# Two-layer graph transformer on one Trainium2 core: two TensorE drains a round as the signal for its products, a new order of the round, gathers that wait only for buffers, and raw rows in layer 2

## The chip, the core and the metric

The kernel runs on one core of one Trainium2 chip. The metric is the device time of one launch in microseconds (us). Engines are named as in the profile: PE is TensorE's matmul, PEld its weight load, DVE is VectorE, ACT is ScalarE, POOL is GpSimd, SP is SyncE. A wait on "PE" below is a wait for a semaphore that a matmul counts up when it ends; a wait on "PE_sequencer" is a wait for one that a drain counts up. A drain is an instruction of TensorE's queue that ends when everything queued before it has ended.

## What is computed

A graph of 6250 nodes with 106250 edges, sorted by target. Two transformer convolutions with two heads of 64 columns, a batch norm with ReLU between them, then residual and layer norm. One convolution, cut to what matters:

```python
q, k, v = h @ Wq + bq, h @ Wk + bk, h @ Wv + bv          # (n, 2, 64)
e = edge_attr @ We                                        # edge_attr: cos(time) 32 | msg 64
alpha = (q[dst] * (k[src] + e)).sum(-1) / 8
a = segment_softmax(alpha, dst)
out = segment_sum((v[src] + e) * a, dst) + h @ Ws + bs
...
h = conv1(x); h = relu((h - mu) / sqrt(var + 1e-5) * bn_g + bn_b)
return layernorm(x + conv2(h))
```

All arithmetic is float32.

## The kernel before

The edges are cut into 105 chunks (NC) of 1024 edges (CE), each holding all edges of at most 64 nodes, so the softmax of a chunk needs nobody else. A chunk is one round of the loop in `conv(c, ...)`; `conv` runs twice, c = 0 for layer 1 and c = 1 for layer 2. `general` is a second program for other graphs, which does not run here.

The order of instructions on every engine is the order in which the Python code issues them (manual schedule). For chunk k the steps are:

- `fetch(k)`: SP loads the edge messages, the chunk's table of products with the queries (`ftab`) and, in layer 2, what layer 1 stored; DVE writes eight code columns (layer 1) or a column of ones (layer 2) into the chunk's tile `ff`. There are six such tiles (AHEAD + 2).
- `gather`: eight indirect DMAs of 128 rows each, issued by POOL, bring the source nodes' rows into `ff`: from `xv_d` in layer 1, in layer 2 from `h_d` (raw output of layer 1) for the first six chunks (RAW) and from `hn_d` (normalised, after ReLU) for the rest.
- `encode`, `sine`, `place` (layer 1): DVE and ACT make the time features; DVE copies them into `ff`.
- `turn_in(k, u)`: TensorE transposes one half of the chunk's rows (`fpx`, and in layer 1 the edge features, `fpe`), ACT copies them to SBUF (`fft`, `fet`).
- `score(k, u)`: two products for each half give the negative logits `fps`. `lowest`: DVE takes the minimum of both halves (`flow`) and the bias `fm`. `weigh`: ACT takes the exponential (`fs`).
- `turn_weights`: TensorE transposes `fs` (`fppt`), ACT copies to `fpt`. `gather_sums`: eight products sum the weighted rows (`fpa`).
- `divide` (DVE: `finv`, `fa`), `finish_turn` (two transposes, `fpo`, and a copy to `fat`), `apply` (products with Wv and We into `fpo`), `finish` (DVE adds the residual; `fres`).

One round k works on four chunks at once: score of k, weights and sums of k-1, division and result of k-2, transposes of k+1. Between the steps the loop pulls from a generator `extra` the side work: in layer 1 the table columns of the remaining twelve blocks of 512 nodes (one product `fpg` and its copy on ACT or DVE), then the rows of h; in layer 2 the tables and residuals of layer 2.

Every consumer waits for the count of the matmul that it needs, and some matmuls wait for PE's own count. Gathers are paced: `tick` is called behind chosen matmuls, and each call lets one gather of the queue go, which waits for that matmul; `allowed` bounds how far ahead. In layer 2 the code of `first_blocks` runs in rounds 0 to 2: it applies ReLU to twelve more blocks of h, transposes them and writes `hn_d`. From chunk 40 (SINGLE) on, layer 1 takes two chunks into one sine, so ACT loads its sine and exponential tables once for two rounds.

Of the kernel before, what the change touches and what calls it, by code (L numbers as in the profile page):

```python
# [1 line left out]

# [11 lines left out]
P = 128  # L14
# [484 lines left out]
class Plan:  # L499
    pass  # L500
# [63 lines left out]
def load_others(nc, pl, const, conv2, bn_g, bn_b):  # L564

    for i, (to, ap) in enumerate(pl.later):
        nc.sync.dma_start(to, ap)
        if i % 2:
            yield
    pl.bs2 = broadcast(nc, const, "fbs2", conv2["bs"], D)  # L570
    yield
    pl.bng = load_column(nc.sync, const, "fbng", bn_g)
    pl.bnb = load_column(nc.sync, const, "fbnb", bn_b)
    yield


def matrices(nc, pl, c, const, bank, brief=None):
# [3 lines left out]
    for i, w in enumerate((wq, wk, web)):  # L581
        pt = bank()
        nc.tensor.transpose(pt, w, pl.ident)
# [10 lines left out]
    for i, kt in enumerate((wkt, wett)):  # L594
        for h in range(H):
            r = slice(h * C, (h + 1) * C)
            pm = bank()
            nc.tensor.matmul(pm, wqt[r, :], kt[r, :], start=True, stop=True)
            a = const.tile([P, P], F32, name=f"fm{c}{h}{i}")
            nc.scalar.activation(a, pm, AF.Copy, scale=-1.0 / C ** 0.5)  # L600
            pb = bank()
            nc.tensor.matmul(pb[:, 0:1], kt[r, :], bq[r, :], start=True, stop=True)
# [22 lines left out]
def tables(nc, pl, c, fT, b0, work, bank):  # L625

    o = work.tile([P, GE, H, 3 - c], F32, name="fo", tag="fo", bufs=1)
    for i, (a, b) in enumerate(pl.mats[c]):
        pg = bank()
        nc.tensor.matmul(pg, a, fT, start=True, stop=True)  # L630
# [33 lines left out]
def ordered(ctx: ExitStack, tc: tile.TileContext, pl, x, dst, edge_attr_64, conv2, bn_g, bn_b, out):  # L664
# [12 lines left out]
    hn_d = dram.tile([N, D], F32, name="hn_d")  # L677
# [20 lines left out]
    SINGLE = 40  # L698

    RAW = 6  # L700

    WIDEN = range(SINGLE - 4, SINGLE)

    def conv(c, extra, first_blocks=None):
# [7 lines left out]
        p_tr = cs.enter_context(tc.tile_pool(name=f"fp_tr{c}", bufs=3, space=bass.MemoryType.PSUM))  # L712
        p_s = cs.enter_context(tc.tile_pool(name=f"fp_s{c}", bufs=3, space=bass.MemoryType.PSUM))
        p_a = cs.enter_context(tc.tile_pool(name=f"fp_a{c}", bufs=1, space=bass.MemoryType.PSUM))
        p_o = cs.enter_context(tc.tile_pool(name=f"fp_o{c}", bufs=1, space=bass.MemoryType.PSUM))
        pl.bank = lambda: p_tr.tile([P, GE], F32, name="fpg", tag="tr")
# [8 lines left out]
        def fetch(k):  # L725
# [16 lines left out]
            s.tab = load.tile([P, NN * H, 3 - c], F32, name="ftab")  # L742
            nc.sync.dma_start(s.tab, pl.tab_d[c][:, bass.ds(s.nb, NN)].rearrange("p n h w -> p (n h) w"))
            if c:
# [4 lines left out]
                s.r = load.tile([NN, D], F32, name="fr", bufs=AHEAD + 3)  # L749
                nc.sync.dma_start(s.r, res_d[bass.ds(s.nb, NN), :])  # L750

        queue = [(k, t) for k in range(NC) for t in range(T)]
        allowed = [-1, False]

        def gather(step):
            k, t = queue.pop(0)
            row = nc.gpsimd.indirect_dma_start(  # L757
                out=ch[k].f[:, t, (1 if c else 0):1 + D], out_offset=None,
                in_=(h_d if k < RAW else hn_d) if c else pl.xv_d,
                in_offset=bass.IndirectOffsetOnAxis(ap=pl.srcs[:, t, k:k + 1], axis=0))  # L760
            if step is not None:
                tc.add_manual_dep(row.ins, step.ins.name, together, reason="gathers keep to the pace of the chunks")
            ch[k].rows.append(row)

        def tick(step, extra=False):
            if queue and queue[0][0] <= allowed[0] and (allowed[1] or not extra):
                gather(step)

        shape = [P, T, TD]

        args, turned = [], []

        def encode(k):
# [3 lines left out]
            if not args:  # L777
                args.append(work.tile([P, 2, T, TD], F32, name="farg"))
            arg = args[0][:, len(args) - 1]
            args.append(k)  # L780
# [11 lines left out]

        def sine():
            arg, *of = args
            args.clear()
            z = work.tile([P, 2, T, TD], F32, name="fzs")
            nc.scalar.activation(z[:, :len(of)], arg[:, :len(of)], AF.Sin, bias=qpi)
            turned.extend((k, z[:, i]) for i, k in enumerate(of))
# [5 lines left out]
        def place():  # L804
            for k, z in turned:
                nc.vector.tensor_copy(ch[k].f[:, :, 1 + D:1 + D + TD], z)
                nc.sync.dma_start(enc_d[k].rearrange("p (t d) -> p t d", d=TD), z)
            turned.clear()

        def turn_in(k, u):  # L810
# [18 lines left out]
            if c:  # L829
                return  # L830
# [8 lines left out]
        def score(k, u):  # L839

            s = ch[k]
            if u == 0:
                s.ps = []
# [560 lines left out]
```

## Time and profile before

| | |
|---|---|
| Median of 3 runs | 2693.82 us (2690.7 to 2695.6) |
| The profiled execution: time, and span from first to last instruction | 2692.01 us, 2690.2 us |
| Mean granted TensorE clock | 0.953 |
| Busy share: PE, PEld, DVE, ACT, POOL | 87%, 64%, 50%, 47%, 60% |

A row of the timeline has the start from the span's beginning, the duration, the engine, the line, the operation, what it writes and reads, how many instructions were merged, and in brackets the engine's idle time ahead of it with what released it. "issue" there is time with no cause that the profile shows, "remote" a release whose sender it could not name. A row of a list of groups has line, engine, operation, tiles, count, then busy us and mean ns of one, then idle time before. A matmul's duration in a row includes the way through the array, so the step from one start to the next is the better measure of what it occupies.

### The profile page before, as it was taken

Reading aid. Unit: us, or ns where it says so; the run is one execution under the profiler, and the core shown is the slowest. Engines: PE = TensorE matmul, PEld = TensorE weight load, DVE = VectorE, ACT = ScalarE, POOL = GpSimd, SP = SyncE. Lnnn points to the kernel's source line nnn. Section 1 sums busy time; section 2 is a strip of 40 time slices with the busy share of each in tenths; the row PEclk is TensorE's granted clock in tenths of the full one; section 3 lists DMA queues with packets and bytes.
Section 4 is the critical chain, followed back from the end, with each engine's and each line's share of the span. In section 5 each row is a group of like instructions: output and inputs, shape, how many; then the busy total and the mean of one; then the engine's idle time right before and its main releaser. Section 6 shows DMA issues by size and latency. Waiting matters only on the chain. (4 is left out here: it accounts for less than half of the span.)

```text
span 2690.2 us, 40319 instructions
## 1 busy us (share of the span) xinstructions
PE 2330.4 (87%) x11482; PEld 1734.9 (64%) x11482; DVE 1331.9 (50%) x4153; ACT 1264.9 (47%) x2147; POOL 1618.3 (60%) x1701
## 2 busy tenths in 40 slices
PE   5898989899898999888957988888898889988887
PEld 3576767667676767767735666666666666666665
DVE  5566666566566666666535433333333333333233
ACT  3666666565555555545523343443334334333344
POOL 3666666666666666666245666666666666666661
PEclk8999999999999999999969999999999999999998
DMA  6455455545555455545365545555555555544451
GB/s 206 143 167 152 140 160 154 149 136 154 161 154 151 136 160 156 153 135 150 103 171 156 143 148 144 138 155 157 153 152 141 151 157 152 153 138 129 132 135 27
DMA packets 239234, 393.49 MB, mean 146 GB/s; under 512 B 62048, under 2 KB 156892, under 8 KB 235676
## 3 DMA queue, kind: packets, MB, share of 16 engines
q1 hardware_dynamic: 166302, 237.60, 29.7%
q0 software_dynamic: 54144, 112.01, 16.4%
q10 hardware_dynamic: 18558, 41.20, 4.3%
q8 instruction: 97, 1.59, 0.2%
q14 instruction: 133, 1.09, 0.1%
HBM read 274.66 MB, written 112.55 MB: 144 GB/s over the span
## 5 line engine op out<-in xcount | busy, mean ns | idle before, releaser
L757 POOL DMA_INDIRECT ff<-xv_d,fsrcs x840 | 808.3, 962 | 482.2 <-issue 172.9
L757 POOL DMA_INDIRECT ff<-hn_d,fsrcs x792 | 758.5, 958 | 434.2 <-issue 167.5
L880 PE MATMUL fpa<-ff,fpt 128*128 128x225 f32 x3360 | 743.0, 377 | 72.6 <-issue 36.9
L880 PEld LDWEIGHTS fpa<-ff,fpt 128*128 128x128 f32 x3360 | 667.7, 205 | 102.1 <-issue 45.4
L828 ACT COPY fft<-fpx 128x512 f32<-128x512 f32 x408 | 240.1, 589 | 627.6 <-PE fpx L820 144.3
L847 PE MATMUL fps<-fft,ftab 128*128 128x512 f32 x840 | 452.0, 620 | 3.1 <-issue 1.8
L854 DVE TENSOR_REDUCE flow<-fps 128x1 f32<-128x512 f32 x420 | 280.6, 685 | 282.4 <-PE fpa L880 99.0
L874 ACT COPY fpt<-fppt 128x512 f32<-128x512 f32 x420 | 228.5, 584 | 329.9 <-remote 71.6
L820 PE MATMUL fpx<-fident,ff 128*128 128x128 f32 x1680 | 263.5, 281 | 24.0 <-issue 15.8
L872 PEld LDWEIGHTS fppt<-fident,fs 128*128 128x128 f32 x1680 | 195.0, 141 | 134.2 <-issue 121.1
L862 ACT ACTIVATE fs<-fps,fm 128x512 f32<-128x512 f32 x420 | 267.4, 692 | 5.2 <-DVE fm L856 2.4
L820 PEld LDWEIGHTS fpx<-fident,ff 128*128 128x128 f32 x1680 | 202.5, 144 | 61.7 <-issue 43.9
L872 PE MATMUL fppt<-fident,fs 128*128 128x128 f32 x1680 | 224.5, 274 | 18.7 <-issue 15.2
L848 PE MATMUL fps<-fet,ftab 112*128 112x512 f32 x420 | 218.8, 602 | 0.0
L944 DVE SCALAR_TENSOR_TENSOR fres<-fpo,fr 64x128 f32<-64x128 f32 x105 | 29.4, 280 | 378.3 <-PE fps L847 107.0
L848 PE MATMUL fps<-fxT,ftab 112*128 112x512 f32 x420 | 216.0, 595 | 0.0
L847 PEld LDWEIGHTS fps<-fft,ftab 128*128 128x128 f32 x840 | 164.3, 227 | 56.6 <-issue 50.5
L903 PEld LDWEIGHTS fpo<-fident,fa 128*128 128x128 f32 x210 | 29.5, 141 | 254.9 <-issue 194.4
L903 PE MATMUL fpo<-fident,fa 128*128 128x128 f32 x210 | 61.9, 295 | 146.7 <-DVE fa L891 92.4
L848 PEld LDWEIGHTS fps<-fet,ftab 112*128 112x128 f32 x420 | 106.0, 253 | 78.3 <-issue 75.6
L835 ACT COPY fet<-fpe 112x512 f32<-112x512 f32 x210 | 124.3, 592 | 57.5 <-PE fpa L880 13.6
L833 PE MATMUL fpe<-fident,ff 128*112 128x128 f32 x840 | 130.4, 279 | 21.6 <-issue 12.9
(217 smaller groups left out, 2559.2 us busy)
## 6 DMA issues: line engine op xcount, KB each, us to landing
fmsg<-in_edge_attr SPq DMA_DIRECT2D x210, 256.0 KB
et_d<-fet SPq DMA_DIRECT2D x105, 448.0 KB
fxT<-et_d SPq DMA_DIRECT2D x105, 448.0 KB
ftab<-tab_d SPq DMA_DIRECT2D x105, 192.0 KB
tab_d<-fo ACTq DMA_DIRECT2D x13, 1536.0 KB
ff<-xv_d,fsrcs POOLq DMA_INDIRECT x840
enc_d<-fzs SPq DMA_DIRECT2D x105, 128.0 KB
ftab<-tab_d SPq DMA_DIRECT2D x105, 128.0 KB
```

The lines of the kernel that those rows point to most:

```text
L757: row = nc.gpsimd.indirect_dma_start(out=ch[k].f[:, t, (1 if c else 0):1 + D], out_offset=None, in_=(h_d if k < RAW else hn_d) if c else p ...
L820: turn = nc.tensor.transpose(px[:, t * P:(t + 1) * P], s.f[:, u * 4 + t, 1:1 + D], ident)
L828: nc.scalar.copy(s.ft[:, u * GE:(u + 1) * GE], px)
L833: turn = nc.tensor.transpose(pe[:EC, t * P:(t + 1) * P], s.f[:, u * 4 + t, 1 + D:], ident)
L835: nc.scalar.copy(s.et[:, u * GE:(u + 1) * GE], pe[:EC])
L847: tick(nc.tensor.matmul(ps, s.tab[:, :, 0], s.ft[:, w], start=True, stop=False))
L848: tick(nc.tensor.matmul(ps, s.tab[:EC, :, 1], s.et[:, w], start=False, stop=True), True)
L854: nc.vector.tensor_reduce(low[:, u:u + 1], s.ps[u], AX.X, OP.min)
L862: nc.scalar.activation(s.s[:, u * GE:(u + 1) * GE], s.ps[u], AF.Exp, bias=s.bias, scale=-1.0)
L872: turn = nc.tensor.transpose(pp[:, t * P:(t + 1) * P], s.s[:, at:at + P], ident)
L874: nc.scalar.copy(s.pt[:, u * GE:(u + 1) * GE], pp)
L880: add = nc.tensor.matmul(s.pa, s.pt[:, t * P:(t + 1) * P], s.f[:, t, 1:1 + D + EW], start=t == 0, stop=t == T - 1)
```

## The change

Four parts, all in `conv` and the generators that it pulls:

1. **Signals.** Each product of TensorE is put into a group (`put`). `drained()` issues a drain and declares it the fence of that group: whoever needs one of these products waits for the drain. There are two a round: one behind `turn_weights(k-1)` and `score(k)`, one behind `turn_in(k+1)` and `finish_turn(k-2)`. The PSUM tiles are fixed: four banks used in turn for transposes and side products, two for scores.
2. **Order of the round.** Both halves of each step stand together. Reading and writing of PSUM are split (`copy_weights`, `copy_in`, `keep_turned`), so copies stand behind the drain. `finish` moves to round k+3, `gather_sums` and `apply` to the round's end. Each side product has one more `yield` between the product and its copy, and the loop pulls twice where it pulled once.
3. **Gathers.** `gather(k + 4)` issues all eight at the top of round k; they wait for the tile `ff` alone. `tick`, `allowed`, SINGLE and WIDEN go. Each chunk has its own sine.
4. **Raw rows.** All chunks of layer 2 gather from `h_d`. ACT applies scale, shift and ReLU as it copies `fft`; DVE's `normalise` runs for all 105 chunks, as two operations (multiply by scale, maximum with -shift) where it was three for six chunks. The missing shift is put back once through the last row of the edge weights. `hn_d`, `relu` and `first_blocks` go; ReLU of a block stands in `block`.

```diff
+        def put(product):
+            group.append(product)
+            return product
+
+        def drained():
+            drain = nc.tensor.drain()
+            name = f"products{c}_{next(fences)}"
+            for product in group:
+                tc.add_to_no_dep_group(name, product.ins)
+            tc.declare_fence(drain.ins, group=name)
+            group.clear()
...
-        def gather(step):
-            k, t = queue.pop(0)
-            row = nc.gpsimd.indirect_dma_start(
-                out=ch[k].f[:, t, (1 if c else 0):1 + D], out_offset=None,
-                in_=(h_d if k < RAW else hn_d) if c else pl.xv_d,
-                in_offset=bass.IndirectOffsetOnAxis(ap=pl.srcs[:, t, k:k + 1], axis=0))
-            if step is not None:
-                tc.add_manual_dep(row.ins, step.ins.name, together, reason="gathers keep to the pace of the chunks")
-            ch[k].rows.append(row)
+        def gather(k):
+            for t in range(T):
+                ch[k].rows.append(nc.gpsimd.indirect_dma_start(
+                    out=ch[k].f[:, t, (1 if c else 0):1 + D], out_offset=None, in_=h_d if c else pl.xv_d,
+                    in_offset=bass.IndirectOffsetOnAxis(ap=pl.srcs[:, t, k:k + 1], axis=0)))
...
-            for i, op in enumerate((OP.mult, OP.add)):
+            for i, op in enumerate((OP.mult, OP.max)):
                 nc.vector.tensor_tensor(rows, rows, pl.spread[:, None, i].to_broadcast([P, T, D]), op)
-            nc.vector.tensor_scalar(rows, rows, 0.0, None, op0=OP.max)
...
                 if on(k + AHEAD):
                     fetch(k + AHEAD)
-                if k == -3:
-                    for _ in range(T + T // 2 if c else 2 * T):
-                        gather(None)
...
+                    gather(k + AHEAD)
...
+                pulls = 0 if k < 0 else 2 if k < 4 or k > 96 else 1
+                if c == 0 and on(k + 1):
+                    place(k + 1)
                 if on(k - 1):
                     turn_weights(k - 1)
...
+                if on(k):
+                    score(k)
+                if group:
+                    drained()
+                if c == 0 and k > 0:
+                    pull()
+                if on(k - 1):
+                    copy_weights(k - 1)
                 if on(k - 2):
                     divide(k - 2)
...
+                if on(k - 3):
+                    finish(k - 3)
                 if on(k):
                     lowest(k)
+                    weigh(k)
+                if on(k + 1):
+                    turn_in(k + 1, 0)
+                    turn_in(k + 1, 1)
+                if c and pulls:
+                    pull()
                 if on(k - 2):
                     finish_turn(k - 2)
+                if group:
+                    drained()
+                if on(k - 2):
+                    keep_turned(k - 2)
                 if on(k + 1):
...
+                    copy_in(k + 1, 0)
+                    copy_in(k + 1, 1)
+                if c and pulls:
+                    pull()
+                if on(k + 2):
+                    settle(k + 2)
+                if c and on(k):
+                    normalise(k)
+                    place(k)
+                if c == 0 and on(k + 2):
+                    encode(k + 2)
                 if on(k - 1):
                     gather_sums(k - 1)
...
                 if on(k - 2):
                     apply(k - 2)
...
+                if c == 0 and pulls:
+                    pull()
```

Three places of the new order. In the rows, a bracket names the semaphores that the instruction waits for (DMASW: gathers, DMAHW: other DMAs; drains have no row of their own).

**TensorE, a round of layer 2 without side work.** Before:

```order
L872 MATMUL fppt<-fident,fs 128x128 [waits PE_49,Activation_49]
L872 MATMUL fppt<-fident,fs 128x128 x3
L872 MATMUL fppt<-fident,fs 128x128 [waits PE_49,Activation_49]
L872 MATMUL fppt<-fident,fs 128x128 x3
L847 MATMUL fps<-fft,ftab 128x512 [waits Activation_49]
L848 MATMUL fps<-fxT,ftab 128x512
L903 MATMUL fpo<-fident,fa 128x128 [waits DVE_49,PE_49]
L904 MATMUL fpo<-fident,fa 128x128
L820 MATMUL fpx<-fident,ff 128x128 [waits DMASW4_49,DMASW5_49,DMASW3_49,DMASW6_49,DMASW2_49,DMASW7_49,DMASW1_49,DMASW0_49]
L820 MATMUL fpx<-fident,ff 128x128 x3
L880 MATMUL fpa<-ff,fpt 128x225 [waits Activation_49]
```

With the change (fpx and fppt are now the banks ftr; the first drain stands behind the second L864, the second behind L919 and its twin):

```order
L888 MATMUL ftr_13833<-fident,fs 128x128 [waits Activation_49]
L888 MATMUL ftr_13833<-fident,fs 128x128 x3
L888 MATMUL ftr_13830<-fident,fs 128x128 [waits Activation_49]
L888 MATMUL ftr_13830<-fident,fs 128x128 x3
L863 MATMUL fps_13834<-fft,ftab 128x512 [waits DMAHW5_49,Activation_49]
L864 MATMUL fps_13834<-fxT,ftab 128x512 [waits DMAHW7_49]
L863 MATMUL fps_13835<-fft,ftab 128x512 [waits Activation_49]
L864 MATMUL fps_13835<-fxT,ftab 128x512
L834 MATMUL ftr_13831<-fident,ff 128x128 [waits DMASW4_49,DMASW5_49,DMASW3_49,DMASW6_49,DMASW2_49,DMASW7_49,DMASW1_49,DMASW0_49]
L834 MATMUL ftr_13831<-fident,ff 128x128 x3
L834 MATMUL ftr_13832<-fident,ff 128x128 x4
L919 MATMUL fpo<-fident,fa 128x128 [waits DVE_49]
```

TensorE no longer waits for its own count, both halves of the scores follow each other, and the transposes of `fa` come behind all transposes of the next chunk.

**VectorE and ScalarE, a round of layer 1.** VectorE before, from the division to the copy of `fpo`:

```order
L888 TENSOR_SCALAR finv<-fpa 128x1
L889 RECIPROCAL finv<-finv 128x1 [waits DVE_49]
L891 TENSOR_SCALAR fa<-fpa,finv 128x225 [waits DVE_49]
L854 TENSOR_REDUCE flow<-fps 128x1 [waits PE_49] x2
L856 TENSOR_SCALAR fm<-flow 128x1 [waits DVE_49]
L906 COPY fat<-fpo 128x256 [waits PE_49]
```

With the change:

```order
L758 TENSOR_SCALAR ff<-fbits 128x8x8 [waits PE_sequencer_49,DVE_49]
L759 CAST ff<-fbits 128x8x8
L820 COPY ff<-fzs 128x8x32 [waits Activation_49]
L905 TENSOR_SCALAR finv<-fpa 128x1
L906 RECIPROCAL finv<-finv 128x1 [waits DVE_49]
L908 TENSOR_SCALAR fa<-fpa,finv 128x225 [waits DVE_49]
L949 TENSOR_TENSOR fres<-fpo,ftab 64x64 [waits DMAHW7_49]
L949 TENSOR_TENSOR fres<-fpo,ftab 64x64
L870 TENSOR_REDUCE flow<-fps_504 128x1
L870 TENSOR_REDUCE flow<-fps_505 128x1
L872 TENSOR_SCALAR fm<-flow 128x1 [waits DVE_49]
L925 COPY fat<-fpo 128x256 [waits PE_sequencer_49]
```

The first drain of the round is awaited by the code columns of `fetch` (their tile was read by the last `gather_sums`), and `fetch`, `place` and `finish` now stand ahead of the minimum. ScalarE before, in the later part of layer 1:

```order
L874 COPY fpt<-fppt 128x512 [waits PE_49,Activation_49]
L874 COPY fpt<-fppt 128x512 [waits PE_49]
L828 COPY fft<-fpx 128x512 [waits PE_49,Activation_49]
L835 COPY fet<-fpe 112x512 [waits DMAHW3_49,PE_49,Activation_49]
L862 ACT_TABLE_LOAD
L862 ACTIVATE fs<-fps,fm 128x512 [waits DVE_49]
L862 ACTIVATE fs<-fps,fm 128x512
```

With the change:

```order
L894 COPY fpt<-ftr_500 128x512 [waits PE_sequencer_49,Activation_49]
L894 COPY fpt<-ftr_501 128x512
L878 ACT_TABLE_LOAD [waits DVE_49]
L878 ACTIVATE fs<-fps_504,fm 128x512 [waits Activation_49]
L878 ACTIVATE fs<-fps_505,fm 128x512
L853 COPY fft<-ftr_502 128x512 [waits PE_sequencer_49,Activation_49]
L854 COPY fet<-ftr_503 112x512 [waits DMAHW4_49,Activation_49]
L853 COPY fft<-ftr_500 128x512
L854 COPY fet<-ftr_501 112x512
L812 ACT_TABLE_LOAD [waits DMAHW7_49,DVE_49]
L812 ACTIVATE fzs<-farg,qpi 128x256 [waits Activation_49]
```

The exponential's table load now carries the wait for VectorE's bias `fm`, so it starts after it; it stands in every round.

**POOL, gathers of layer 2.** Before, and with the change:

```order
L757 DMA ff<-hn_d,fsrcs 128x128 [waits DMASW2_49,PE_49]
L757 DMA ff<-hn_d,fsrcs 128x128 [waits DMASW3_49,DVE_49,PE_49]
L757 DMA ff<-hn_d,fsrcs 128x128 [waits DMASW4_49,PE_49]
L757 DMA ff<-hn_d,fsrcs 128x128 [waits DMASW5_49,PE_49]
L757 DMA ff<-hn_d,fsrcs 128x128 [waits DMASW6_49,PE_49]
```

```order
L772 DMA ff<-h_d,fsrcs 128x128 [waits DMASW2_49]
L772 DMA ff<-h_d,fsrcs 128x128 [waits DMASW3_49,PE_sequencer_49,DVE_49]
L772 DMA ff<-h_d,fsrcs 128x128 [waits DMASW4_49]
L772 DMA ff<-h_d,fsrcs 128x128 [waits DMASW5_49]
L772 DMA ff<-h_d,fsrcs 128x128 [waits DMASW6_49]
```

One gather of eight waits for a drain, the other seven only for the gather that used their semaphore last.

257 lines of the change are left out of this document (126 added, 131 removed).

## The prediction

> **What bounds the kernel now.** I read the timeline of TensorE first, for the length of a round, then the timeline of all engines around a stall, then the same in a stretch without gathers, then the groups by line for durations. `gather_sums` occurs once a round, so its first row of each layer and its last give the rounds:
>
> ```profile
> 85.85 3.21 PE L880 MATMUL fpa<-ff,fpt 128*128 128x225 f32 x16
> ...
> 1341.79 3.21 PE L880 MATMUL fpa<-ff,fpt 128*128 128x225 f32 x16
> ...
> 1408.02 4.29 PE L880 MATMUL fpa<-ff,fpt 128*128 128x225 f32 x11
> ...
> 2667.53 4.89 PE L880 MATMUL fpa<-ff,fpt 128*128 128x225 f32 x16
> ```
>
> 104 steps each: layer 1 takes (1341.79 - 85.85)/104 = 12.08 us a round, layer 2 (2667.53 - 1408.02)/104 = 12.11. What TensorE needs is less. Near the end of layer 1, where no side work is pulled, its starts are:
>
> ```profile
> 1317.38 3.21 PE L880 MATMUL fpa<-ff,fpt 128*128 128x225 f32 x16
> 1320.42 0.60 PE L820 MATMUL fpx<-fident,ff 128*128 128x128 f32 x4
> ...
> 1321.29 0.39 PE L913 MATMUL fpo<-fat,fwv 128*128 128x128 f32 x2
> ...
> 1321.74 1.08 PE L847 MATMUL fps<-fft,ftab 128*128 128x512 f32 x2
> 1322.66 1.02 PE L848 MATMUL fps<-fet,ftab 112*128 112x512 f32 x2
> 1323.52 1.04 PE L872 MATMUL fppt<-fident,fs 128*128 128x128 f32 x8
> 1324.40 1.08 PE L847 MATMUL fps<-fft,ftab 128*128 128x512 f32 x2
> ...
> 1327.27 3.21 PE L880 MATMUL fpa<-ff,fpt 128*128 128x225 f32 x16
> ```
>
> From start to start: sums 3.04, eight transposes 0.87, `apply` 0.45, a product with 512 columns 0.92 or 0.86, eight transposes of weights 0.88; the whole round 1327.27 - 1317.38 = 9.89. So some 2 us of each round are not work. The next stretch shows what they are:
>
> ```profile
> 1893.39 1.04 PE L872 MATMUL fppt<-fident,fs 128*128 128x128 f32 x8
> ...
> 1893.94 0.28 DVE L944 SCALAR_TENSOR_TENSOR fres<-fpo,fr 64x128 f32<-64x128 f32 x1 [5.24 <-PE fppt L872]
> ...
> 1896.29 0.63 PE L820 MATMUL fpx<-fident,ff 128*128 128x128 f32 x4
> ...
> 1899.75 1.07 ACT L874 COPY fpt<-fppt 128x512 f32<-128x512 f32 x2 [4.10 <-remote]
> 1899.84 0.69 DVE L854 TENSOR_REDUCE flow<-fps 128x1 f32<-128x512 f32 x1 [2.33 <-remote]
> 1899.93 0.95 POOL L757 DMA_INDIRECT ff<-hn_d,fsrcs  x1 [1.63 <-remote]
> 1900.39 1.87 PE L880 MATMUL fpa<-ff,fpt 128*128 128x225 f32 x4 [3.47 <-issue]
> ```
>
> The transposes of the weights ended at 1893.39 + 1.04 = 1894.43, and ACT, idle, copies them at 1899.75, 5.3 us later. ACT, DVE and POOL are released together within 0.2 us, while TensorE has stood since 1896.92 waiting for that copy. Nobody worked: the matmuls' counts came late and in one burst. Where no gathers run, they do not:
>
> ```profile
> 1304.75 1.07 ACT L874 COPY fpt<-fppt 128x512 f32<-128x512 f32 x2 [2.42 <-PE fps L847]
> 1304.79 0.94 POOL L757 DMA_INDIRECT ff<-xv_d,fsrcs  x1 [1.35 <-PE fps L847]
> ...
> 1305.11 0.16 DVE L888 TENSOR_SCALAR finv<-fpa 128x1 f32<-128x1 f32 x1
> ...
> 1305.50 0.45 DVE L891 TENSOR_SCALAR fa<-fpa,finv 128x225 f32<-128x225 f32 x1
> ...
> 1305.87 1.28 DVE L854 TENSOR_REDUCE flow<-fps 128x1 f32<-128x512 f32 x2
> ...
> 1307.18 0.21 DVE L856 TENSOR_SCALAR fm<-flow 128x1 f32<-128x1 f32 x1
> ...
> 1308.25 1.28 ACT L862 ACTIVATE fs<-fps,fm 128x512 f32<-128x512 f32 x2
> ...
> 1310.52 0.60 PE L820 MATMUL fpx<-fident,ff 128*128 128x128 f32 x4
> ...
> 1311.16 0.59 ACT L828 COPY fft<-fpx 128x512 f32<-128x512 f32 x1 [1.62 <-PE fpx L820]
> ```
>
> The gather at 1304.79 is the last of layer 1. After it the transposes end at 1311.12 and ACT copies at 1311.16, 0.04 us later, and the rounds run at 9.89. So the kernel is bound by TensorE's signals being held while POOL gathers; ACT's signal came at once even in the burst (the first copy ends near 1900.29, TensorE starts at 1900.39).
>
> **The change part by part.** *Signals.* A drain's signal is not in this trace. Its delay lies between 0.04 (no gathers) and 5.3 us (the stall). I take 0.05, because it is TensorE's queue and not the matmul that counts, and the other engines' counts, like ACT's above, are not held; both ends stay for the range. The drain itself costs TensorE the way through the array that otherwise overlaps (L848: 1.02 long, next start 0.86 later, so 0.16) and a restart (0.1, as at 1900.39): 0.26, with the signal about 0.3. Below zero it cannot be, since a drain does no work; above, I allow 0.65, one whole product of 512 columns (0.59) waited out. By the Trainium skill (PSUM — Partial Sum Buffer, Engine vs sequencer instructions) a drain is a true completion signal because it waits for the engine to go fully idle; no run here shows one yet, and by that rule the 0.16 is paid each time and nothing can hide it.
>
> *Order, layer 1.* The groups by line of layer 1 give the other durations:
>
> ```profile
> L862 ACT ACT_TABLE_LOAD x68 | 87.2, 1283 | 1.2
> L931 DVE TENSOR_TENSOR fres<-fpo,ftab 64x64 f32<-64x64 f32 x194 | 49.5, 255 | 105.6 <-PE fppt L872 35.5 <-PE fps L847 29.1 <-PE fpo L914 14.8
> L806 DVE COPY ff<-fzs 128x256 f32<-128x256 f32 x98 | 29.1, 323 | 59.6 <-ACT fzs L797 35.8 <-issue 23.5
> L634 ACT ACTIVATE fo<-fpg,fb 128x512 f32<-128x512 f32 x22 | 25.9, 1175 | 7.3 <-PE fppt L872 4.9 <-PE fpg L630 2.2 <-PE fps L847 0.2
> L740 DVE TENSOR_SCALAR ff<-fbits 128x64 f32<-128x64 int32 x97 | 25.7, 265 | 3.3
> L741 DVE CAST ff<-fbits 128x64 f32<-128x64 int32 x97 | 24.6, 254 | 0.0
> ```
>
> From the first drain's signal (0), for which the code columns now wait with all of DVE's round queued behind them: DVE does code columns 0.27 + 0.25, place 0.32 (0.9 with the latency), divide 0.84 (1305.11 to 1305.95; 1.75), finish 2 x 0.26 (2.3), minimum 1.28 and bias 0.21 (3.8). Only then ACT loads its table, 1.28 (5.15), and takes two exponentials, 1.28 (6.45). TensorE: four transposes, then twelve more once place is done at 0.9 (2.3); `finish_turn` writes the PSUM tile that `finish` reads, so it waits for 2.3 and ends at 2.6; second drain, 2.85; sums 3.04 (5.9), apply (6.35), weights 0.88 (7.2; the exponential allows 6.95), scores 2 x 1.78 (10.75), drain: 11.0. The second drain's consumers are late anyway (ACT is in the exponential until 6.45), so its signal costs nothing. A side product adds 0.92: 11.9. Its copy now stands ahead of the rest: on ACT 1.18 ahead of the weights' copies, whose two banks the last edge transposes need again (0.6 more, since TensorE reaches them 0.6 before), on DVE about the same length ahead of divide (1.1 more). A block of twelve takes seven rounds: 11.9, 12.5, 12.5, 13.0, 13.0, 12.1 and 11.0, mean 12.3; the other twenty rounds, with the rows of h, I put at 11.6 between 11.0 and 12.3. Layer 1: 12.15, which is 104 x 0.07 = 7 us more. The extra sine table load each round lies behind the copies on ACT, which has ended by then (6.45 + 4 x 0.59 = 8.8 of 11).
>
> *Order, layer 2.* No code columns, no table: divide is done at 0.95, fres (0.28) at 1.25, `finish_turn` ends near 1.6, drain 1.85, sums 4.9, apply 5.4, weights 6.3 (the exponential ends at 4.8), scores 9.8, drain 10.0. A side product adds 0.92 less the wait for fres that it fills: 10.5. Sixty of 105 rounds have one: 10.3. The copies for layer 2 lie behind ACT's and DVE's work of the round and have 3 us of room.
>
> *Gathers and raw rows.* POOL, when nothing holds it, and beside `normalise`:
>
> ```profile
> 1357.32 0.94 POOL L757 DMA_INDIRECT ff<-h_d,fsrcs  x1 [0.30 <-issue]
> 1358.57 0.95 POOL L757 DMA_INDIRECT ff<-h_d,fsrcs  x1 [0.30 <-issue]
> ...
> 1397.63 1.62 POOL L757 DMA_INDIRECT ff<-h_d,fsrcs  x1 [10.10 <-PE fps L847]
> ...
> 1422.54 2.49 DVE L896 TENSOR_TENSOR ff<-ff,fspread 128x1024 f32<-128x1024 f32 x2
> ...
> 1423.40 1.19 POOL L757 DMA_INDIRECT ff<-h_d,fsrcs  x1 [0.30 <-issue]
> ```
>
> One gather each 1.25 us makes 8 x 1.25 = 10.0 a round, now a floor close to TensorE's 10.3. What DVE does in layer 2 today, in a table of stretches (length; then busy us and count of PE, PEld, DVE, ACT, POOL; clock, DMA share, GB/s):
>
> ```profile
> 1660.00:1960.00 300.00, 264.72 (x1303) 190.41 (x1302) 108.75 (x371) 114.78 (x239) 189.61 (x199) 0.95 0.54 151
> ```
>
> DVE is busy 108.75 of 300, or 4.4 of 12.11 us a round. `normalise` adds 2.49, which leaves it at 6.9 of 10, and lengthens a gather beside it by 0.24 (1.19) to 0.67 (1.62): 10.2 to 10.7. I take 10.5 for layer 2, which is 104 x (12.11 - 10.5) = 167 us less. `first_blocks` goes with it; its rounds are in the 12.11. The spare work (a later `finish`, start, change of layers) I leave at nothing, with 10 us either way.
>
> Sum against the profiled span: 2690.2 + 7 - 167 = 2530; the profiled run's time was 1.8 above its span and the median of the runs 1.8 above that: 2534, said as **2530**.
>
> **The rivals.** *Slower: the drain's signal is held like the matmul's.* All DVE and ACT work and, through place or fres, TensorE hang on the first drain, so a mean delay h costs 208 x h. It decides from h = 160/208 = 0.8 us; at 1.5, 2845. For it: SP, DVE, ACT and POOL all saw TensorE late; against: only matmuls were seen to count late. *POOL is shut out during `normalise`*: 10.0 + 2.49 = 12.5 in layer 2, 104 x 0.4 = 41 us more, 2740; the rows above lengthen by a quarter of that. The Trainium skill (SBUF — State Buffer, SBUF: two separate sides) states that rule, an exclusive lock between GpSimd and two-input VectorE work; the trace agrees only in part, 0.24 and 0.67 of 2.49. *Drains cost 0.65*: 416 x 0.35 = 146 more, 2675. *Layer 1's copies are hidden after all*: 11.0 + 0.92 x 5/7 x 0.8 = 11.5, 70 us less, 2460. *The signals change nothing*, because gathers themselves slow the round: 2690.
>
> **How the numbers follow.** Forecast 45%, held signals 17%, hidden copies 15%, dear drains 12%, shut-out POOL 6%, nothing 5%. Runs of this kernel tell 0.2% from no change. Faster: 45 + 15 + 10 = 70%; within 0.2%: 3%; slower: 17 + 6 + 4 = 27%. The range 2410 to 2745 leaves out most of the held signals and the end of the hidden copies. The forecast's own range is 2480 to 2590.
>
> **What would show it.** Right: copies start within 0.2 us of a drain, no releases "remote" after TensorE has ended; rounds of 11 to 13 us in layer 1 and 10 to 10.7 in layer 2; POOL idle 0.30 between gathers. Wrong: idle ACT and DVE for over 0.8 us after a drain's last product, or gathers of over 1.2 us throughout layer 2.

## The result, and the profile after: slower by 9%

| | before | after |
|---|---|---|
| Median, us | 2692.26 (4 runs) | 2949.28 (4 runs, 2927.61 to 2958.13) |
| Ratio, 95% interval | | 1.0943 [1.0879, 1.1007] |
| Profiled execution: time, span, clock | 2692.01, 2690.2, 0.953 | 2954.61, 2952.6, 0.932 |

Forecast was 2530, between 2410 and 2745. The rounds first, from the timeline of TensorE of the kernel after: the first product of `gather_sums` (now L900) in the first and last round of each layer.

```profile
124.53 0.45 PE L900 MATMUL fpa<-ff,fpt 128*128 128x225 f32 x1
...
1456.10 0.46 PE L900 MATMUL fpa<-ff,fpt 128*128 128x225 f32 x1
...
1548.66 0.45 PE L900 MATMUL fpa<-ff,fpt 128*128 128x225 f32 x1
...
2931.19 0.45 PE L900 MATMUL fpa<-ff,fpt 128*128 128x225 f32 x1
```

The start takes 124.5 in place of 85.9 (+39), a round of layer 1 12.80 in place of 12.08 (+75 over 104), the change of layers 92.6 in place of 66.2 (+26), a round of layer 2 13.29 in place of 12.11 (+123), the end 1 less: +262, the whole difference of the spans. The lower mean clock is no cause of its own: the step from one score product to the next is 0.43 us in both traces. Every stage that was to stay got longer, and layer 2 with them.

The groups of the page after (line, engine, operation, count; busy and mean; then idle time ahead and what ended most of it; L782 is the drain):

```profile
PE 2390.7 (81%) x11435; PEld 1735.1 (59%) x11435; DVE 1506.5 (51%) x4336; ACT 1363.5 (46%) x2240; POOL 1637.3 (55%) x1701
...
L772 POOL DMA_INDIRECT ff<-h_d,fsrcs x840 | 825.9, 983 | 647.5 <-DVE finv L906 324.7
...
L894 ACT COPY fpt<-ftr 128x512 f32<-128x512 f32 x420 | 226.5, 591 | 845.9 <-PEq L782 779.2
...
L905 DVE TENSOR_SCALAR finv<-fpa 128x1 f32<-128x1 f32 x210 | 31.4, 150 | 544.6 <-issue 528.0
...
L758 DVE TENSOR_SCALAR ff<-fbits 128x64 f32<-128x64 int32 x105 | 21.4, 204 | 436.4 <-PEq L782 434.3
```

ACT and DVE wait for the drain, and POOL for DVE's first steps behind it. A wait for a drain is no fault by itself; what matters is when TensorE's last product had ended. A steady round of layer 2, from the timeline of all engines:

```profile
1897.14 0.94 POOL L772 DMA_INDIRECT ff<-h_d,fsrcs  x1 [2.27 <-DVE finv L906]
...
1906.10 0.94 POOL L772 DMA_INDIRECT ff<-h_d,fsrcs  x1 [0.30 <-issue]
...
1906.53 1.02 PE L864 MATMUL fps<-fxT,ftab 112*128 112x512 f32 x2
...
1908.73 0.15 DVE L905 TENSOR_SCALAR finv<-fpa 128x1 f32<-128x1 f32 x1 [4.99 <-issue]
...
1908.77 1.07 ACT L894 COPY fpt<-ftr 128x512 f32<-128x512 f32 x2 [6.31 <-PEq L782]
...
1909.21 1.06 PE L834 MATMUL ftr<-fident,ff 128*128 128x128 f32 x8 [1.66 <-DMA ff<-h_d,fsrcs]
1909.42 0.94 POOL L772 DMA_INDIRECT ff<-h_d,fsrcs  x1 [2.37 <-DVE finv L906]
...
1911.08 0.27 PE L920 MATMUL fpo<-fident,fa 128*128 128x128 f32 x1
...
1911.43 2.96 PEld L900 LDWEIGHTS fpa<-ff,fpt 128*128 128x128 f32 x16 [0.31 <-issue]
...
1911.69 0.41 DVE L925 COPY fat<-fpo 128x256 f32<-128x256 f32 x1
```

The first drain's last product ends at 1906.53 + 1.02 = 1907.55; DVE, ACT and TensorE itself go on at 1908.7 or later. (The row of TensorE names a DMA, but the rows of that chunk were gathered three rounds earlier.) The second drain, two gathers into the next train, lets TensorE go on 0.08 us after its product (1911.35). The eight gathers start from 1897.14 to 1906.10; the signal comes 2.6 us after the last start, the next train 0.7 after the signal: 8.96 + 2.6 + 0.7 = 12.3, and 1909.42 - 1897.14 = 12.28. The train holds the signal that lets the next train go. In layer 1 the same drain comes 2.84 us after the train's last start and is not late:

```profile
507.57 0.94 POOL L772 DMA_INDIRECT ff<-xv_d,fsrcs  x1 [0.30 <-issue]
...
509.39 1.02 PE L864 MATMUL fps<-fet,ftab 112*128 112x512 f32 x2
...
510.47 1.07 ACT L894 COPY fpt<-ftr 128x512 f32<-128x512 f32 x2 [2.96 <-PEq L782]
```

Where a train gets longer than eight, the hold can too. In six rounds of layer 2 the second drain falls into a train of eleven or twelve and is held 3.1 to 10.3 us. The longest of these holds (the last product ends at 2195.84 + 0.27 = 2196.11):

```profile
2195.84 0.27 PE L920 MATMUL fpo<-fident,fa 128*128 128x128 f32 x1
...
2202.97 0.94 POOL L772 DMA_INDIRECT ff<-h_d,fsrcs  x1 [0.30 <-issue]
...
2206.49 0.43 DVE L925 COPY fat<-fpo 128x256 f32<-128x256 f32 x1 [9.99 <-PEq L782]
...
2206.51 5.93 PE L900 MATMUL fpa<-ff,fpt 128*128 128x225 f32 x16 [10.40 <-issue]
```

And at the start of layer 1 the first 48 gathers, which wait for nothing, follow each other: ACT's first copy starts 37.8 us after its transposes ended at 67.79.

```profile
66.73 1.06 PE L842 MATMUL ftr<-fident,ff 128*112 128x128 f32 x4
...
105.58 0.58 ACT L853 COPY fft<-ftr 128x512 f32<-128x512 f32 x1 [40.98 <-PEq L782]
```

The trace records the end of every drain; the end of a product in a trace is modelled, but in runs where nothing is held (below) every drain ends 0.02 to 0.05 us behind it. From the end of the last product ahead of it, the 457 drains of this kernel took 293 us, 84 of them over 1 us; 302 took under 0.1. Count as one train the gathers that start within 2 us of each other: of 186 drains whose last product ended among the first five gathers of a train, none took over 0.25 us; of 61 that came later in one, 48 took over 0.3. Of all 113 that took over 0.3 us, 94 ended 2.25 to 3.0 us after a train's last start; eight ended before it, among them two of the longest, 11.7 and 14.1 us, in the 48 gathers at the change of layers.

### The profile page after: what moved, and what is told of

Read it like the earlier page. It is cut to its first block, busy times and chain, and to the rows that moved or that the text cites. A ratio compares the mean times of both kernels' runs of the same rounds, so it can differ in the third digit from the quotient of the medians.

```text
span 2952.6 us, 39328 instructions
## 1 busy us (share of the span) xinstructions
PE 2390.7 (81%) x11435; PEld 1735.1 (59%) x11435; DVE 1506.5 (51%) x4336; ACT 1363.5 (46%) x2240; POOL 1637.3 (55%) x1701
## 5 line engine op out<-in xcount | busy, mean ns | idle before, releaser
L772 POOL DMA_INDIRECT ff<-h_d,fsrcs x840 | 825.9, 983 | 647.5 <-DVE finv L906 324.7
L900 PE MATMUL fpa<-ff,fpt 128*128 128x225 f32 x3360 | 751.1, 380 | 96.9 <-issue 81.7
L900 PEld LDWEIGHTS fpa<-ff,fpt 128*128 128x128 f32 x3360 | 664.7, 203 | 163.1 <-issue 145.8
L894 ACT COPY fpt<-ftr 128x512 f32<-128x512 f32 x420 | 226.5, 591 | 845.9 <-PEq L782 779.2
L834 PE MATMUL ftr<-fident,ff 128*128 128x128 f32 x1680 | 254.8, 287 | 256.8 <-DMA ff<-h_d,fsrcs 128.5
L834 PEld LDWEIGHTS ftr<-fident,ff 128*128 128x128 f32 x1680 | 191.8, 146 | 420.3 <-issue 405.4
L913 DVE TENSOR_TENSOR ff<-ff,fspread 128x1024 f32<-128x1024 f32 x210 | 256.3, 1221 | 3.6
L888 PE MATMUL ftr<-fident,fs 128*128 128x128 f32 x1680 | 230.2, 280 | 13.5 <-issue 11.6
L888 PEld LDWEIGHTS ftr<-fident,fs 128*128 128x128 f32 x1680 | 188.0, 142 | 60.4 <-issue 41.9
L864 PE MATMUL fps<-fxT,ftab 112*128 112x512 f32 x420 | 217.2, 598 | 0.7 <-issue 0.7
L864 PE MATMUL fps<-fet,ftab 112*128 112x512 f32 x420 | 216.3, 596 | 0.0
L851 ACT ACTIVATE fft<-ftr,fshift,fscale 128x512 f32<-128x512 f32 x210 | 152.0, 781 | 101.0 <-PEq L782 99.2
L925 DVE COPY fat<-fpo 128x256 f32<-128x256 f32 x210 | 87.5, 417 | 140.5 <-PEq L782 134.3
L842 PE MATMUL ftr<-fident,ff 128*112 128x128 f32 x840 | 132.5, 281 | 23.8 <-DVE finv L905 11.6
```

What stands on the lines that cost most here:

```text
L772: ch[k].rows.append(nc.gpsimd.indirect_dma_start(out=ch[k].f[:, t, (1 if c else 0):1 + D], out_offset=None, in_=h_d if c else pl.xv_d, in_ ...
L834: step = put(nc.tensor.transpose(px[:, t * P:(t + 1) * P], s.f[:, u * 4 + t, 1:1 + D], ident))
L842: put(nc.tensor.transpose(pe[:EC, t * P:(t + 1) * P], s.f[:, u * 4 + t, 1 + D:], ident))
L851: nc.scalar.activation(s.ft[:, w], px, AF.Relu, bias=pl.shift, scale=pl.scale)
L864: put(nc.tensor.matmul(scores[u], s.tab[:EC, :, 1], s.et[:, w], start=False, stop=True))
L888: put(nc.tensor.transpose(pp[:, t * P:(t + 1) * P], s.s[:, at:at + P], ident))
```

## The experiments

Theory: TensorE's signals, a drain's as well as a matmul's count, are held while gathers follow each other. Rivals: drains or the new order are dear by themselves; raw rows shut POOL out. Ratios are to the kernel before on the same chip, which took 2690 to 2722 us, except on one chip, below.

**Without gathers**, changed kernel, before, and changed kernel without drains:

```diff
-            for t in range(T):
+            for t in range(T if k < AHEAD + 2 else 0):
```

> The changed kernel with the gathers of the first six chunks of each layer alone (it leaves out all others; later chunks reuse those six tiles). Held-signal theory: every drain behind them done within 0.1 us of its last product, rounds 11.2 without and some 12.1 with side work in layer 1, 10.5 and some 10.8 in layer 2; 2560 to 2650. Rival (drains and new order are dear by themselves, whether or not gathers run): 2850 or more.

> The kernel before with the gathers of the first six chunks of each layer alone (it leaves out all others). Held-signal theory: matmul counts come at once, rounds fall from 12.1 to 9.9 without and some 10.7 with side work, 86 + 208 x 10.7 + 66 + 23 = 2400, between 2350 and 2450. Against the changed kernel without gathers this gives the price of drains and order by themselves, some 200 us, nearly all in layer 1. Rival (the gathers cost nothing here, the rounds are bound by the chain of steps): within 30 us of 2690.

> The same without the drains: consumers wait for the matmul's own count. What it saves against the changed kernel without gathers is the price of two drains a round where no signal is held. By my prediction's 0.3 us each, 457 drains: 60 to 140 us less. If the drains owe their price to held signals alone: less than 40.

Measured 2634.94 (0.9794 [0.9769, 0.9819]), 2319.95 (0.8612 [0.8594, 0.8629]) and 2337.19 (0.8687 [0.8665, 0.8709]). So the gathers behind the first 48 of each layer cost the kernel before 2694.95 - 2319.95 = 375 us and the changed kernel 314. Rounds fall from 12.08 and 12.11 to 10.54 and 10.01 in the kernel before, and to 11.84 and 11.18 in the changed one, where all drains behind the first 48 gathers take under 0.1 us. But the second rival is right too: without drains the same kernel takes 298 us less, over twice the upper end of what I expected, so drains with everything queued on them are dear also where nothing is held: rounds of layer 2 without side work take 10.07 us with two drains and 9.23 without, rounds of layer 1 with it 12.1 to 13.7 against 10.7. Against the kernel before without gathers, order and raw rows together cost 17 us.

**Drains alone, and gathers split in two.** In the first, products are no longer put into a group, so no drain is issued; in the second, gathers 0 to 3 wait for the first drain and 4 to 7 for the second.

```diff
-            group.append(product)
```
```diff
+                if after is not None:
+                    tc.add_manual_dep(ch[k].rows[-1].ins, after.ins.name, together, ...)
...
-                    gather(k + AHEAD)
...
+                sign = drained() if group else None
+                if on(k + AHEAD):
+                    gather(k + AHEAD, 0, sign)
```

> The changed kernel without its drains: every consumer waits for the matmul's own count again, order, gathers and raw rows as changed. Held-signal theory: the counts are held by the same trains of eight gathers, so most of the loss stays, 2800 to 3000. Rival (the drain is what costs: 457 of them at 0.6 us): 270 us less, 2680 or less.

> The changed kernel with its eight gathers of a round split: four wait for the first drain, four for the second. In the changed kernel's trace a drain that fell within the first four gathers of a train was done at once, one behind the fifth or a later one was held. If it is the place in the train that decides: all drains behind the start within 0.2 us, rounds of 12.1 and 10.8, 2560 to 2680. Rival (a signal is held whenever gathers run without a longer pause, and here they run nearly all the time): 2850 to 3050, drains held in most rounds. Rival (drains and order dear): no change, 2950.

Without drains 2729.41 (1.0148 [1.0109, 1.0187]): 220 of the 257 us are the drains', outside both ranges and nearer the rival's. Counts are still held: of the products that end during a train or in the 2.7 us behind its last start, 33% show a count within 0.15 us, in the kernel before 28%. But a held count does not stop TensorE's own queue, a held drain does. The split gave 2884.73 (1.0703 [1.0684, 1.0722]) but says nothing on the place in the train: the second drain follows the first by some 2.8 us, so four and four still made trains of eight, with the first drain of layer 2 held 0.95 us on average. It gained at the start (first sums at 100.8).

**Raw rows alone**, in the kernel before:

```diff
-    RAW = 6
+    RAW = NC
...
-            for i, op in enumerate((OP.mult, OP.add)):
+            for i, op in enumerate((OP.mult, OP.max)):
...
-                if c and k in range(3):
-                    first_blocks(k)
```

> The kernel before with raw rows throughout layer 2 and nothing else of the change: ReLU in the copy of fft and in block, two-operation normalise for all chunks, no hn_d. Held-signal theory: normalise lengthens two gathers a round by 0.1 to 0.2 us, the first three rounds of layer 2 lose their extra work (some 15 us), so 2660 to 2710. Rival (POOL is shut out while normalise runs, 2.49 us a round): 2740 or more.

Measured 2747.6 (1.0222 [1.0196, 1.0249]), the rival's number, but not by its mechanism. Gathers of layer 2, before, then with raw rows (POOL, busy us and mean ns):

```profile
L757 POOL DMA_INDIRECT ff<-hn_d,fsrcs x792 | 758.5, 958 | 434.2 <-issue 167.5 <-PE fpa L880 55.8 <-PE fpx L820 42.0
```
```profile
L757 POOL DMA_INDIRECT ff<-h_d,fsrcs x840 | 840.3, 1000 | 529.5 <-issue 182.0 <-PE fpx L820 79.2 <-PE fpa L880 69.5
```

A gather is 42 ns longer on average, 8 x 0.042 = 0.34 us a round; POOL shut out for 2.49 would show 0.31 on each. The round grew by 0.50; the rest of it is open.

**Start, ReLU, and both without drains.** The first edit spreads the gathers of chunks 2 to 5; the second lets the generator yield twice between a block's ReLU and its first product.

```diff
-                    gather(k + AHEAD)
+                    if k < -2 or k > 2:
+                        gather(k + AHEAD)
...
+                    if k < 3:
+                        gather(k + 3, ch[k + 1].step)
```
```diff
             next(res)
+            yield
+            yield
             yield from tables(nc, pl, 1, ...)
```

> The changed kernel without drains, and with the gathers of chunks 2 to 5 of each layer waiting for the transposes of chunks 0 to 3, so that no layer begins with 48 gathers in one train. Without drains alone it took 2729; its first sums came 33 us later than before, and the change of layers took 29 us longer. Held-signal theory (a signal waits until the train has been worked off): both go, 2729 - 60 = 2670, between 2655 and 2695. Rival (the start is late for another reason, such as the loads or the new order of the first rounds): no change, 2720 to 2735.

> The changed kernel with the ReLU of a block of nodes in layer 2 one round ahead of the product that reads it. In the changed kernel without gathers, TensorE stood 4.05 us in front of that product in one round of about seven, and with it the second drain; rounds of 16 us without gathers, 18 to 21 with. Theory (the ReLU, queued on ACT behind the exponentials, costs 5 to 6 us for each of twelve blocks): 2949 - 65 = 2885, between 2865 and 2905. Rival (those long rounds are the held second drain alone): within 15 us of 2949.

> The changed kernel without drains, with the gathers of the first chunks spread as in the run before and the ReLU a round ahead: what of the change is left is order, raw rows and gathers that wait for buffers. Theory: 2715 less 12 x 5 = 2655, between 2630 and 2690, the first version under the kernel before (2692). Rival (the long rounds of layer 2 come from held counts): 2700 to 2730.

The first gave 2714.83 (1.0075 [1.0051, 1.0099]). First sums came at 89.0 (119.4) and the change of layers took 56.3 (90.7), so the trains of 48 were the cause there; but rounds went from 12.04 and 11.98 to 12.22 and 12.43, and of 65 us 15 are left. Why the rounds grew is not settled; the profiled execution, 2730.12, was the slowest of ten. The ReLU gave 2917.10 (1.0710 [1.0663, 1.0756]) on a chip 1% slower than the first, outside the range in us. By ratio it is 63 us under the 1.0943 of the changed kernel and 51 under the 1.0901 of its repetition; by rounds of layer 2, 12.86 against 13.29 and 13.44, 45 and 60 us. So it is worth 45 to 63 us of the 65 expected. The changed kernel without gathers shows what it was:

```profile
1628.62 0.68 ACT L880 ACTIVATE fs<-fps,fm 128x512 f32<-128x512 f32 x1
1629.19 0.81 ACT L1161 ACTIVATE fhT<-fhT,fshift,fscale 128x512 f32<-128x512 f32 x1
...
1630.06 2.07 PE L644 MATMUL ftr<-fhT,fm 128*128 128x512 f32 x2 [4.05 <-ACT fhT L1161]
```

TensorE stands 4 us for a ReLU that ACT reaches behind both exponentials, and the second drain with it. All three together without drains gave 2728.83 beside 2720.10 (1.0028 [1.0006, 1.0049]): not under the kernel before, so the 2655 was wrong; its counts are still held (33% at once).

**Loads in place of gathers, and slower gathers.**

```diff
-                ch[k].rows.append(nc.gpsimd.indirect_dma_start(...))
+                ch[k].rows.append(nc.sync.dma_start(
+                    ch[k].f[:, t, (1 if c else 0):1 + D], (h_d if c else pl.xv_d)[t * P:(t + 1) * P, :]))
```
```diff
+                for _ in range(3):
+                    nc.gpsimd.memset(idle, 0.0)
```

> The changed kernel with every gather replaced by a plain load of 128 rows of the same size from SP's queue (it leaves out the choice of rows). Without gathers behind the sixth chunk it took 2635, with them 2949. Theory that POOL's gathers hold TensorE's signals: every drain is done within 0.1 us of its last product, the start and the change of layers shrink too, 2560 to 2680. Rival (the traffic to the tiles holds them, whoever issues it): drains late as with gathers, 2850 or more.

> The changed kernel with three small memsets on POOL behind every gather, so that gathers start some 1.7 to 1.8 us apart in place of 1.25. If signals are held because gathers are issued faster than they are worked off (a train of 8 is worked off 2.65 us after its last start, one of 48 5.6 to 7.9 us after it, so some 1.33 us each): drains within 0.2 us, POOL sets the round at 14 to 15 us, 3150 to 3250. Rival (held whenever POOL gathers, at any rate): the first drain still waits for the end of the train, rounds of 14 + 2.6 + 0.7 = 17 us, 3600 or more.

With loads 2604.10 (0.9565 [0.9518, 0.9612]), first sums at 74.2, rounds of 12.15 and 11.38. Slower gathers 3294.25 (1.2100 [1.2039, 1.2161]), bound by POOL. In both, every drain was done within 0.05 us, while on the same chip the changed kernel with the ReLU a round ahead had 89 of 457 over 1 us. The slower gathers, timeline of all engines (their median step is 1.77 us; the last one here waited longer, for DVE):

```profile
1900.65 0.95 POOL L772 DMA_INDIRECT ff<-h_d,fsrcs  x1 [0.16 <-issue]
1901.61 0.66 POOL L776 MEMSET fidle<- 128x96 f32 x3
1902.82 0.95 POOL L772 DMA_INDIRECT ff<-h_d,fsrcs  x1 [0.55 <-DVE finv L909]
```
```profile
1901.33 1.02 PE L867 MATMUL fps<-fxT,ftab 112*128 112x512 f32 x2
...
1902.43 0.15 DVE L908 TENSOR_SCALAR finv<-fpa 128x1 f32<-128x1 f32 x1 [3.82 <-issue]
1902.45 0.07 DVE L753 MEMSET ff<- 128x8 f32 x1
1902.47 1.07 ACT L897 COPY fpt<-ftr 128x512 f32<-128x512 f32 x2 [5.93 <-PEq L784]
```

The product ends at 1902.35, DVE starts at 1902.43. So neither the drain by itself nor traffic of this size holds: POOL's gathers do, at a start each 1.25 us, and not at 1.77. The drains of these kernels, counted from the traces:

```
kernel                  drains  under 0.1 us  over 1 us  sum, us
changed                    457           302         84      293
changed, repeated          457           282         79      313
four and four              457           300         87      231
without later gathers      457           453          4       86
loads for gathers          457           457          0       10
gathers 1.77 us apart      457           457          0       10
```

**A pace that costs little.** One memset of 96 or 256 columns behind each gather, in the kernel before, and of 96 in the changed kernel and in the last one without drains:

```diff
+            nc.gpsimd.memset(idle, 0.0)
```

> The kernel before with one memset of 96 columns (0.19 us in the run with three) on POOL behind every gather, nothing else. With three of them behind each gather every drain of the changed kernel was done at once, gathers 1.77 us apart. Pace theory (TensorE's signals are held because gathers start every 1.25 us, faster than the 1.33 us in which I estimate them to be worked off): 0.95 + 0.22 + 0.16 = 1.33 apart, counts come at once, POOL needs 10.7 a round, rounds of some 11.0 in place of 12.1: 2692 - 208 x 1.1 = 2460, between 2420 and 2560. Rival (1.33 is still too fast): within 30 us of 2692. Rival (the gathers hold signals whatever the pace, and the three memsets only made room for them): slower by 8 x 0.08 x 208 = 130 us.

> The same with a memset of 256 columns, so gathers start some 1.42 us apart and POOL needs 11.4 a round. Pace theory: counts at once, rounds of 11.5, 2692 - 208 x 0.6 = 2570, between 2530 and 2620, slower than with the short memset if that one suffices, faster if it does not.

> The changed kernel with one memset of 96 columns on POOL behind every gather. Pace theory: all drains prompt, also in the trains of 48 at the start and the change of layers, which come 60 us earlier; rounds as without gathers (11.9 and 11.2, over POOL's 10.7): 2635 - 60 = 2575, and some 50 for waits on landings: between 2560 and 2660. That is my forecast for the change (2530) with the held signals taken away. Rival (1.33 is still too fast): 2900 or more.

> The changed kernel without drains, with spread first gathers and the ReLU a round ahead (the run before: as fast as the kernel before), and one memset of 96 columns behind every gather. Pace theory: rounds near POOL's 10.7, 94 + 104 x 11 + 63 + 104 x 11 + 20 = 2465, between 2420 and 2540. Rival (still too fast): 2700 to 2740.

These four fell on a chip where the kernel before takes 2325.70 (2317.62 to 2332.33, 7 runs). They took 2421.95 (1.0420 [1.0381, 1.0459]), 2635.43 (1.1339 [1.1298, 1.1379]), 2613.89 (1.1236 [1.1202, 1.1270]) and 2385.68 (1.0253 [1.0214, 1.0292]). Two of the four times lie in their ranges (2421.95 and 2613.89), but not for the expected cause: on this chip counts (98 to 99% within 0.15 us) and all drains come at once with a memset, and the kernel before, without one, is as quick there as it is elsewhere without gathers. What the chip shows is the change with prompt signals in both kernels at one pace: 2614 against 2422, 8% slower. The last three runs went to chips like the others:

> The kernel before with one memset behind every gather once more, because the chip of the last four runs took 2326 us for the kernel before itself, where the others took 2690 to 2720. Where the kernel before takes some 2692 beside it: pace theory 2420 to 2480, as on the other chip, since no count is held in either; rival (1.33 us is still too fast) 2660 to 2850. Where it takes 2326: 2422 again, and the question stays open.

> The changed kernel, unchanged, beside it. Where the kernel before takes some 2692: 2949 again. Where it takes 2326: no drain held by more than 0.1 us, rounds as with plain loads (12.0 and 11.3), 85 + 104 x 12.0 + 62 + 104 x 11.3 + 21 = 2590, between 2550 and 2620, so slower than before by 11% where its signals are prompt as well.

> The kernel before with the memset of 256 columns behind every gather once more, gathers some 1.44 us apart. At 1.25 and 1.33 us counts were held on four chips (prompt in 28% and 26%), at 1.77 none, on a fifth chip none at 1.33 and 1.44. Where the kernel before takes some 2700 beside it: if the gathers are worked off in 1.32 to 1.38 us each (release 2.65 us after the last of 8, 5.6 to 7.9 after the last of 48), counts come at once and the time is near the 2635 of the other chip, 2610 to 2670, faster than before. Rival (the limit lies between 1.44 and 1.77): 2760 or more. Where it takes 2326: 2635 again, and the limit stays open.

The median step with a memset of 96 columns is 1.31 us, not the 1.33 that was expected, and with 256 columns 1.44. Measured 2735.07 beside 2721.79 (1.0055 [1.0034, 1.0075]), 2966.01 (1.0901 [1.0874, 1.0928]) and 2694.38 beside 2689.69 (1.0024 [1.0008, 1.0040]). ACT's wait ahead of the copies of the weights (groups by line; busy and mean, then idle) tells held from prompt counts, the memset of 96 columns on the one chip and on the other:

```profile
L876 ACT COPY fpt<-fppt 128x512 f32<-128x512 f32 x420 | 224.1, 585 | 136.6 <-PE fppt L874 132.6 <-ACT fo L632 1.7 <-PE fps L850 0.8
```
```profile
L876 ACT COPY fpt<-fppt 128x512 f32<-128x512 f32 x420 | 229.4, 584 | 355.0 <-PE fpx L822 83.0 <-remote 80.0 <-PE fpa L882 66.9
```

On the first the copies wait for their own transposes (L874) alone. At 1.31 us, then, the counts are held as at 1.25 (27% at once); at 1.44 about as often (31% at once), but the kernel is only 59 us behind the other chip, where at 1.31 it was 313 and at 1.25 364 to 396. Part of that POOL's own 11.5 us a round covers. So a memset between gathers does not free the signals by itself. Together with the run at 1.77 us this says that the pace decides, with a limit between 1.44 us (the kernel before) and 1.77 (the changed one), where POOL alone needs over 11.5 us a round and little or nothing is left to gain. No version here that does all the work beats the kernel before.

## Why the prediction was wrong

**What bounds the kernel before** was read rightly: some 2 us of every round lost to counts held during gathers; without gathers it takes 375 us less, in rounds of 10.54 and 10.01.

**The signal of a drain** is the step that failed: "I take 0.05, because it is TensorE's queue and not the matmul that counts". It is held by the same gathers. The mean over the first drains was 0.25 us in layer 1 and 0.90 in layer 2, over the second 0.31 and 0.50, with 38 us at the start and 38 at the change of layers. The trace of before could not show a drain, and the end that I took of the two, 0.04 and 5.3, was argued, not measured. That SP also saw TensorE late stood there as a sign for the rival, and should have weighed more than that only matmuls had been seen.

**The rival of held signals** was the right mechanism with 17%. Its decision point, 0.8 us, was passed: (2949 - 2534)/208 = 2.0 by its price. The first drains' own mean is lower, 0.58 us over both layers, by the price 120 of the 160 us that decide; the rest is what the price left out: the second drain, which it took as covered, and POOL, whose next train waits for the signal that the last one holds, 12.28 where POOL alone needs 10.0.

**Order and drains, layer 1**: predicted 12.15 with prompt signals; 11.84 without gathers, 12.15 with loads. **Layer 2**: predicted 10.5; 11.18 and 11.38. Rounds without side work are as in the sum (10.0 forecast, 10.1 to 10.3), but "the copies for layer 2 lie behind ACT's and DVE's work of the round" overlooked that a block's product waits for its ReLU: 12 x 5 us, and 45 to 63 measured. The price of the drains lay inside these rounds; against the same kernel with counts it is 298 us, not the 416 x 0.3 = 125 that one gets from the drain alone. That is 0.7 us a drain, over the 0.65 that the prediction allowed at most. Rounds without side work lose 0.84 us to two drains and the others more; that the copy of a side product and the chain behind the drain come one after another is argued, not tested.

**Gathers and raw rows**: 983 ns a gather in place of 958 are 0.2 us a round, the lower end of the 0.2 to 0.7. `first_blocks` saved little: raw rows alone are slower by 2.2%.

**Start and change of layers** "I leave at nothing": +39 and +26, both from 48 gathers in one train. With loads in place of gathers the kernel takes 0.9565 of before, 2575; less the ReLU, 2512 to 2530, where 2534 was forecast with prompt signals. That the two are so close is in part luck: with loads the start and the change of layers are 21 us shorter than before, which the sum did not have, and rounds of layer 2 with a side product take some 11.2 us where it had 10.5. The rest, 2949 - 2575 = 374 us, goes with the gathers. And the sum set prompt signals after against held ones before: where they are prompt in both, at one pace on the other chip, the change is 8% slower.

## What to carry to other kernels

A signal that arrives late need not be late because of the instruction that sends it: before replacing it by another from the same engine, find what it is late behind, here by leaving the gathers out of one run. Making more work hang on such a signal, and its own engine first, turns a delay that was partly covered into one that is paid in full; above all where the cause of the delay waits for the signal in turn. And compare on one chip: the same kernel took 2690 to 2722 us on some and 2326 on another.

## Not expected of the hardware

On five of six chips TensorE's signals are held while POOL starts an indirect gather of 128 rows each 1.25 to 1.44 us. A drain is held mostly from the sixth gather of a train on, until some 2.6 us after the last start (after 48 gathers 5.6 and 7.9, with two releases inside such a train), up to 37.7 us in one case. At 1.77 us they are not held, nor with plain loads of as many rows. One chip of the six did not hold them at 1.31 and 1.44 us, and ran the kernel before, which starts one each 1.25, at 2326 us; why is open, and so is the place in the chip where they wait.
